# A row comparison on VectorE reads the row's number from one PSUM column in place of an SBUF constant

## Chip, cores and metric

The kernel runs on one core of a Trainium2 chip. The metric is the device time of one execution in microseconds (us). The kernel before takes 5775.4 us, the median of three runs (5774.86 to 5783.15). A profiled execution is told of separately below, because its own time is another one.

## What is computed

One message-passing layer of a graph network, with 12,500 nodes of 128 features and 412,500 edges that are sorted by `dst`. Each edge has a `src`, a `dst`, 20 attributes and a weight. Cut to what matters (ssp is softplus less log 2):

```python
h   = relu(layernorm(x)) @ W_in2f                        # 12500 x 128
Wij = (ssp(f_ij @ W_f1 + b_f1) @ W_f2 + b_f2) * rcut[:, None]
x_ij = h[dst] * Wij                                      # one row of 128 for each edge
agg = segment_sum(x_ij, src, num_segments=12500)
out = x + ssp(agg @ W_o1 + b_o1) @ W_o2 + b_o2
```

So the rows of h are picked by `dst`, which is sorted, and the products are added up by `src`, which is in no order.

## The kernel before

**Chunks and groups.** The edges are worked on in 806 chunks of 512 (`CH`), four to a group. Four tiles of 128 edges make up a chunk. A software pipeline, written out by hand in `step(k)`, takes one step for each chunk; every engine's instructions stand in the order in which `step` issues them, and nothing reorders them later. In step k the several stages work on different chunks: `blocks` on chunk k+7, `rank` on k+6, `hidden` on k+4, `window` on k+2, `value`, `pick` and `picked` on k+1, and `message` on k.

**Picking the rows of h.** As `dst` is sorted, the 512 edges of a chunk need rows out of a short window of 32 rows. h is held in DRAM in three bf16 parts, so a window is 96 rows (`WP = 3 * 32`) of 128. `rel` (96 partitions by 512 edges, bf16) has for each edge the distance of its `dst` from the window's first row, the same in each partition. The constant `prow` has in partition p the number p // 3, the row to which partition p belongs. `window` (line 748) compares the two on VectorE and so makes `at`, a matrix of zeros and ones. In `pick` (line 775) TensorE multiplies the four 96 by 128 pieces of `at` with the window `near`, into the PSUM tile `picked`. `picked` (line 783) lets ScalarE move it to `hg` in SBUF, times the edge's weight.

**Values and messages.** `hidden` (lines 658 to 662) and `hidden_end` (line 673) make the first layer of the filter net for two chunks at once, `bias` (line 760) has ScalarE write the second bias into the PSUM tile `v`, and `value` (line 767) adds the second layer to it on TensorE. `message` (line 794) multiplies `v` by `hg` on VectorE into `o`; before it, once in two chunks, line 792 copies 8 columns into a fresh buffer of `o`, of which there are four, each for two chunks.

**Slots and scatters.** `blocks` (line 678), `rank` (lines 697 and 729) and `rank_end` (line 702) work out for each edge a slot of its own in a DRAM table of its source's block of 128 nodes. `message` then has GpSimd scatter each tile of 128 rows of `o` to those slots, with one indirect DMA (line 798): four scatters to a chunk, 3224 in all. GpSimd does nothing else once the constants are made.

**Collecting.** The edges are cut into seven segments with a table each. When a segment is done, `Collect` reads its table back (`m`), compares the node in each row with the numbers 0 to 127 (`compare`, line 847) and sums the rows by a matmul (`add`, line 860), between the steps of later segments; the last segment is collected after the last step, together with the output layers. The numbers 0 to 127 of lines 678 and 847 lie in a PSUM tile, `count_ps` (allocated at line 536, and filled by ScalarE at line 1052 from the SBUF constant `places`).

**The constants.** `constants` (from line 251) makes `prow` before all of that: an iota of 96 by 512 on GpSimd (line 269), a shift on VectorE (line 294), and a copy to bf16 (line 295).

Of the kernel before, what the change touches and what calls it, by code (L numbers as in the profile page):

```python
# [9 lines left out]
F32 = mybir.dt.float32  # L10
BF16 = mybir.dt.bfloat16
F16 = mybir.dt.float16
I32 = mybir.dt.int32
AF = mybir.ActivationFunctionType
ALU = mybir.AluOpType
PSUM = bass.MemoryType.PSUM

P = 128
TG = 16
CH = 512  # L20
# [21 lines left out]
def gnn_kernel(  # L42
# [20 lines left out]
    nc = tc.nc  # L63
# [52 lines left out]
    def sbuf(name, shape, dtype=F32):  # L116
        return const.tile(shape, dtype, name=name)
# [6 lines left out]
    NC = NG * NCHUNK  # L124
    NPART = ceil_div(NC, P)
    WP = 3 * WR
# [15 lines left out]
    bf2, bo2 = (sbuf(n, [P, P]) for n in ("bf2", "bo2"))  # L142
    before = sbuf("before", [P, P])
    spare = sbuf("spare", [P, 1])
    prow = sbuf("prow", [WP, CH], BF16)
    ones = sbuf("ones", [P, 1])
    flag = sbuf("flag", [1, 1], I32)
    after = sbuf("after", [P, P], F16)
# [18 lines left out]
    early_room = state.tile([P, NTILE * P], F32, name="early_room", tag="agg")  # L167
# [4 lines left out]
    rows_at = NPART * CH * 3 // 2 + CH  # L172
# [4 lines left out]
    def early_row(k):  # L177
        return early_room[0:1, rows_at + k * NC:rows_at + (k + 1) * NC]

    first = early_row(0).bitcast(I32)  # L180
    base, last_w, strays, kept_in = (early_row(k) for k in range(1, 5))

    def load_x(q):
        n = min(QT, NTILE - q * QT)
        full = min(n, N // P - q * QT)
        xb = ln.tile([P, QT, P], F32, name="xb")
        if full < n:
            nc.vector.memset(xb[:, full:n, :], 0.0)
            nc.sync.dma_start(xb[:N % P, full, :], x[q * QN + full * P:N, :])
        if full:  # L190
            nc.sync.dma_start(xb[:, :full, :], x[q * QN:q * QN + full * P, :]
                              .rearrange("(c p) f -> p c f", p=P))
        return xb


    def first_load(i):
        h = heads[i]
        nc.sync.dma_start(first[:, h], dst_c[h, 0:1].rearrange("c o -> o c"))

    def bounds(i):  # L200

        h = heads[i]
        c0 = h.start
        while c0 < h.stop:
            t = table_of[c0]
            c1 = next((c for c in range(c0, h.stop) if table_of[c] != t), h.stop)
            nc.gpsimd.memset(base[:, c0:c1], float(tables[t][0]))
            nc.gpsimd.memset(last_w[:, c0:c1], float(tables[t][1] - WR))
            c0 = c1
# [11 lines left out]
    def part_load(k):  # L221
        c0, n = parts_c[k]
        nc.sync.dma_start(dc[k][:n, :], dst_c[c0:c0 + n, :])
# [27 lines left out]
    def constants():  # L251

        early[0] = load_x(0)
        part_load(0)
        first_load(0)
        nc.sync.dma_start(win, w_in2f)

        for j in range(NCHUNK):
            nc.sync.dma_start(wf1[32 * j:32 * j + RBF, :], w_f1)

        nc.scalar.preload_act_table_set("natural_log_exp_and_others")
        nc.scalar.dma_start(bf1, b_f1[:, None])
        nc.scalar.dma_start(wf2, w_f2)
        nc.scalar.dma_start(bf2, b_f2[None, :].to_broadcast([P, P]))
        make_identity(nc, ident)
        bounds(0)

        prow_i = early_room[:WP, rows_at + 5 * NC:rows_at + 5 * NC + CH].bitcast(I32)
        nc.gpsimd.iota(prow_i, pattern=[[0, CH]], base=0, channel_multiplier=43)
        nc.gpsimd.iota(places, pattern=[[1, P]], base=0, channel_multiplier=0,  # L270
                       allow_small_or_imprecise_dtypes=True)

        nc.gpsimd.memset(after, 1.0)
        nc.gpsimd.affine_select(out=after, in_=after, compare_op=ALU.is_ge, fill=0.0, base=-1,
                                pattern=[[1, P]], channel_multiplier=-1)
        nc.gpsimd.memset(zero, 0.0)

        nc.gpsimd.memset(before, 1.0)
        nc.gpsimd.affine_select(out=before, in_=before, compare_op=ALU.is_ge, fill=0.0, base=-1,
                                pattern=[[-1, P]], channel_multiplier=1)  # L280
        nc.gpsimd.iota(spare, pattern=[[1, 1]], base=N, channel_multiplier=1,
                       allow_small_or_imprecise_dtypes=True)
        bounds(1)
        nc.vector.memset(eps, EPS)
        nc.vector.memset(half, 0.5)
        nc.vector.memset(bad, 0.0)
        nc.vector.memset(rel[:, NPART - 1, :], 0.0)
        nc.vector.memset(ones, 1.0)
        nc.vector.memset(none, 0.0)
        nc.vector.memset(ones_b, 1.0)  # L290

        for t in range(QT):
            nc.vector.memset(turn[:, :, t:t + 1], -1.0 if t % 2 else 1.0)
        nc.vector.tensor_scalar(prow_i, prow_i, 7, None, op0=ALU.logical_shift_right)
        nc.vector.tensor_copy(prow, prow_i)
        nc.vector.scalar_tensor_tensor(after, ident, BIG, after, op0=ALU.mult, op1=ALU.add)

        nc.vector.tensor_scalar(rest_of, after, -1.0, 1.0, op0=ALU.mult, op1=ALU.add)
# [226 lines left out]
    with tc.tile_pool(name="edge", bufs=2) as edge, tc.tile_pool(  # L525
        name="quad", bufs=3
# [6 lines left out]
        free = state_ps.tile([P, CH], F32, name="free")[:, :QB]  # L533
        free_v = free.rearrange("p (t b) -> p t b", b=NBLK)

        count_ps = state_ps.tile([P, P], F32, name="count_ps")

        def clear(seg):

# [30 lines left out]
        class Group:  # L570
# [174 lines left out]
            def window(self, c):  # L745

                at = quad.tile([WP, CH], BF16, name="at")
                nc.vector.tensor_tensor(at, self.rel[:, c, :], prow, op=ALU.is_equal)  # L748
                self.at_w = at

            def bias(self, c):
# [232 lines left out]
        at = [seg.c1 + 9 for seg in segs[:-1]]  # L984
# [64 lines left out]

        with tc.manual_schedule():  # L1050
            constants()
            nc.scalar.activation(count_ps, places, AF.Copy)
            h = [make_h(q, psum) for q in range(2)]
            next(h[0])
            relative(0)
            shift(0)
            next(h[0])
            next(h[0])
            aside = side()

            start = {-9: (1, 0), -7: (2, 0), -6: (0, 1), -5: (1, 1)}
            start |= {k: (0, 1) for k in range(-4, 1)}
            for k in range(-LG, max(NCH, max(units) + 1)):
                for seg, d in zeros.get(k, ()):
                    seg.clears.append(nc.sync.dma_start(*d).ins.name)
                now = units.get(k, ())
                for c, u in now:
                    if u == 0:
                        for i in range(AHEAD):
                            c.load(i)  # L1070
                step(k, now)
                if k == -LG:
                    early[1] = load_x(1)
                for m, n in zip(h, start.get(k, (0, 0))):
                    for _ in range(n):
                        next(m, None)
                if k == -6:
                    biases(psum)
                if k >= 0:
                    next(aside, None)  # L1080
            summed[0].add(summed[1])
            summed[0].keep()
            worst = state.tile([1, 1], F32, name="worst")
            nc.vector.tensor_reduce(worst, bad, axis=mybir.AxisListType.X, op=ALU.max)
            nc.vector.tensor_copy(flag, worst)


            last = collects[-1]
            outs = []
            for b in range(0, NBLK, QT):  # L1090
                n = min(QT, NBLK - b)
                sT = kept["agg"][:, b:b + n, :].rearrange("p c f -> p (c f)")
                outs.append(finish(b, n, sT, quad, psum))

            def go(q):
                if 0 <= q < NQ:
                    next(outs[q], None)

            go(0)
            for u in range(AHEAD):  # L1100
                last.load(u)
            last.compare(0)
            q = 0
            for u in range(len(last.units)):
                last.load(u + AHEAD)
                if u + 1 < len(last.units):
                    last.compare(u + 1)
                if last.kept:
                    last.kept = []
                    go(q - 4)  # L1110
                last.add(u)
                if last.done:
                    last.keep()
                    go(q + 1)
                    go(q - 1)
                    go(q - 2)
                    go(q - 3)
                    go(q - 4)
                    q += 1
            for q in range(NQ, NQ + 5):  # L1120
                go(q - 4)
                go(q - 1)
                go(q - 2)
                go(q - 3)
                go(q - 4)

    missed = nc.values_load(flag[0:1, 0:1], min_val=0, max_val=P)
    with tc.If(missed > 0):
        with tc.tile_pool(name="any_e", bufs=2) as edge, tc.tile_pool(
            name="any_q", bufs=2  # L1130
# [51 lines left out]
```

## Time and profile before

| | |
|---|---|
| median of three runs | 5775.4 us |
| the profiled execution's own time | 4263.65 us |
| its span, from the first to the last instruction | 4261.9 us |
| TensorE busy | 3383.1 us, 79% of the span |
| VectorE busy | 3176.8 us, 75% |
| GpSimd busy | 3124.7 us, 73% |
| ScalarE busy | 2674.3 us, 63% |
| granted clock of TensorE, mean | 0.819 |
| first and last scatter start | 40.9 us and 4140.7 us |

A profiled execution is one run of the program with the hardware profiler on. Busy times, waits and durations below are from it alone, and they add up to its own time of 4263.65 us, not to the median: the profiled execution took 1512 us less than the runs that are timed without a profile. In a row of instruction groups there stand the line of the kernel, the engine, the operation, the tiles (out<-in), the shapes and the number of instructions; then the busy time in us and the mean of one in ns; then the idle time of the engine just before them, and what ended most of it.

### The profile page before, as it was taken

To read this page: it belongs to the slowest core of one execution; us is meant where nothing else is said; L and a number is where in the kernel's file an instruction comes from. 1 tells how busy PE (TensorE), PEld (TensorE's weight loads), DVE (VectorE), ACT (ScalarE), POOL (GpSimd) and SP (SyncE) were. 2 spreads that over 40 slices of the span, in tenths; PEclk is the share of its full clock that TensorE was granted. 3 is DMA by queue.
4 is the path that set the end of the run, shared out by engine and by line. 5 is a ranking of instruction groups with operands and counts; after the bars stand their busy time and mean duration, and the time that the engine had idled before them with its cause. 6 is when DMAs were issued, how large, how long until landed. Compare 5 with 4: busy or idle time off the path is not lost. (4 is left out here: it accounts for less than half of the span.)

```text
span 4261.9 us, 71875 instructions
## 1 busy us (share of the span) xinstructions
PE 3383.1 (79%) x21574; PEld 2590.7 (61%) x21574; DVE 3176.8 (75%) x6676; ACT 2674.3 (63%) x5489; POOL 3124.7 (73%) x3292
## 2 busy tenths in 40 slices
PE   6676677767777767788888888888888988988978
PEld 3444444445444444467767777777776777777767
DVE  7776666666555555667778878888888988988968
ACT  5776666666666666666666666666665666665635
POOL 5777777777777777777777777777777777777760
PEclk8867667676655665579999999999998999989989
DMA  6665655654444454467787777887787768877767
GB/s 192 189 192 166 184 172 158 180 161 137 131 124 126 120 163 123 113 183 211 232 269 206 217 208 213 248 244 212 214 238 240 234 193 269 239 203 203 196 180 223
DMA packets 515676, 820.79 MB, mean 193 GB/s; under 512 B 177170, under 2 KB 312966, under 8 KB 515282
## 3 DMA queue, kind: packets, MB, share of 16 engines
q1 hardware_dynamic: 411682, 602.85, 49.9%
q0 software_dynamic: 103168, 213.15, 15.1%
q8 instruction: 176, 2.88, 0.3%
q14 instruction: 218, 1.79, 0.1%
q10 hardware_dynamic: 432, 0.13, 0.0%
HBM read 419.09 MB, written 396.64 MB: 191 GB/s over the span
## 5 line engine op out<-in xcount | busy, mean ns | idle before, releaser
L798 POOL DMA_INDIRECT slots<-o,slot x3224 | 3117.8, 967 | 1016.2 <-issue 786.0
L767 PE MATMUL v<-wf,r 128*128 128x128 f32 x6448 | 1124.5, 330 | 374.9 <-ACT v L760 373.5
L767 PEld LDWEIGHTS v<-wf,r 128*128 128x128 f32 x6448 | 997.5, 236 | 679.4 <-ACT v L760 675.1
L760 ACT ACTIVATE v<-bf 128x512 f32<-128x512 f32 x804 | 477.5, 594 | 1387.8 <-DVE o L794 1384.1
L860 PEld LDWEIGHTS acc<-to,m 128*128 128x128 f32 x8132 | 1052.2, 207 | 348.3 <-DVE agg L883 120.7
L860 PE MATMUL acc<-to,m 128*128 128x128 f32 x8132 | 1125.4, 296 | 121.4 <-DVE agg L883 59.4
L783 ACT ACTIVATE hg<-picked,rcut 128x128 f32<-128x128 f32 x3224 | 905.5, 362 | 61.8 <-PE picked L775 59.3
L658 PE MATMUL z<-f,wf 20*128 20x512 f32 x1612 | 559.7, 771 | 336.4 <-DVE r L673 299.6
L673 DVE SCALAR_TENSOR_TENSOR r<-z,nbf,a 128x1024 f32<-128x1024 f32 x403 | 516.8, 1282 | 331.9 <-ACT a L667 331.4
L847 DVE TENSOR_TENSOR to<-count_ps,m 128x512 f32<-128x512 f32 (+3 forms) x824 | 642.6, 804 | 84.4 <-DMA m<-slots 61.2
L702 DVE TENSOR_REDUCE top<-free 128x4 f32<-128x392 f32 x806 | 448.8, 557 | 232.2 <-PE free L697 229.7
L794 DVE TENSOR_TENSOR o<-v,hg 128x512 f32<-128x512 f32 x806 | 549.8, 682 | 54.3 <-ACT hg L783 53.7
L658 PEld LDWEIGHTS z<-f,wf 20*128 20x128 f32 x1612 | 151.7, 217 | 522.5 <-issue 256.3
L667 ACT ACTIVATE a<-a,half 128x1024 f32<-128x1024 f32 x403 | 467.6, 1160 | 0.0
L661 ACT ACTIVATE a<-z,bf 128x1024 f32<-128x1024 f32 x403 | 455.1, 1129 | 9.6 <-PE z L658 9.6
L678 DVE TENSOR_TENSOR inb<-count_ps,blk 128x392 f16<-128x392 f32 x806 | 446.9, 554 | 0.0
L662 ACT ACTIVATE a<-a 128x1024 f32<-128x1024 f32 x403 | 425.9, 1057 | 12.8
L775 PE MATMUL picked<-near,at 96*128 96x128 bf16 x3224 | 377.0, 250 | 0.0
L729 PE MATMUL free<-inb,rest_of 128*128 128x392 f16 x806 | 322.1, 400 | 15.7 <-DVE top L702 15.7
L748 DVE TENSOR_TENSOR at<-rel,prow 96x512 bf16<-96x512 bf16 x806 | 332.9, 413 | 0.0
L697 PE MATMUL free<-inb,after 128*128 128x392 f16 x806 | 319.4, 396 | 3.3 <-DVE used L735 3.1
L775 PEld LDWEIGHTS <-at 96*128 96x128 bf16 x3224 | 303.7, 115 | 29.9
(109 smaller groups left out, 1141.1 us busy)
## 6 DMA issues: line engine op xcount, KB each, us to landing
m<-slots SPq DMA_DIRECT2D x311, 387.0 KB
m<-slots SPq DMA_DIRECT2D x317, 258.0 KB
rel<-rel_d SPq DMA_DIRECT2D x202, 384.0 KB
m<-slots SPq DMA_DIRECT2D x172, 322.5 KB
slots<-o,slot POOLq DMA_INDIRECT x3224
slots<-zero SPq DMA_DIRECT2D x96, 387.0 KB
slots<-zero SPq DMA_DIRECT2D x64, 516.0 KB
f<-in_f_t SPq DMA_DIRECT2D x404, 80.0 KB
```

Of the source, the lines that this page charges most:

```text
L658: nc.tensor.matmul(z[:, k, :], wf1[rows, :], self.f[rows, :], start=True, stop=True)
L661: nc.scalar.activation(a, z, AF.Abs, bias=bf1)
L667: nc.scalar.activation(a, a, AF.Ln, bias=half, scale=0.5)
L673: nc.vector.scalar_tensor_tensor(r, z, nbf1, a, op0=ALU.max, op1=ALU.add)
L760: nc.scalar.activation(v, spread(bf12, QT), AF.Copy)
L767: nc.tensor.matmul(v[:, i, :], r[:, i * P:(i + 1) * P], wf2, start=False, stop=True, skip_group_check=True)
L775: nc.tensor.matmul(ps[:, i, :], at[:, i * P:(i + 1) * P], near, start=i == 0, stop=i == QT - 1, skip_group_check=True)
L783: nc.scalar.activation(hg[:, i, :], ps[:, i, :], AF.Copy, scale=self.rcut[:, j:j + 1])
L794: nc.vector.tensor_mul(o[:, :, :P], v, hg)
L798: put = nc.gpsimd.indirect_dma_start(out=views[j % VIEWS], out_offset=bass.IndirectOffsetOnAxis(ap=self.slot[:, j:j + 1], axis=0), in_=o[: ...
L847: nc.vector.tensor_tensor(to[:, :n, :], count_ps[:, None, :].to_broadcast([P, n, P]), self.m[u][:, :n, P:].to_broadcast([P, n, P]), op=ALU ...
L860: nc.tensor.matmul(self.acc[b // QT][:, i, :], m[:, j, :P], to[:, j, :], start=t == 0, stop=t == self.seg.tiles(b) - 1)
```

## The change

`prow` shrinks from 512 columns of bf16 to one column of fp32. The PSUM tile `count_ps` is allocated with one more column, and after line 1052 ScalarE copies `prow` to that column, `prow_ps`. `window` then compares `prow_ps`, spread over 512 edges with a step of zero, with `rel`. The first operand thus comes from PSUM, and only the second from SBUF. On no engine does the order of the instructions differ; ScalarE has one more.

```diff
-    prow = sbuf("prow", [WP, CH], BF16)
+    prow = sbuf("prow", [WP, 1])
...
-        prow_i = early_room[:WP, rows_at + 5 * NC:rows_at + 5 * NC + CH].bitcast(I32)
-        nc.gpsimd.iota(prow_i, pattern=[[0, CH]], base=0, channel_multiplier=43)
+        prow_i = early_room[:WP, rows_at + 5 * NC:rows_at + 5 * NC + 1].bitcast(I32)
+        nc.gpsimd.iota(prow_i, pattern=[[0, 1]], base=0, channel_multiplier=43)
...
-        count_ps = state_ps.tile([P, P], F32, name="count_ps")
+        counts = state_ps.tile([P, P + 1], F32, name="count_ps")
+        count_ps, prow_ps = counts[:, :P], counts[:WP, P:]
...
             def window(self, c):
                 at = quad.tile([WP, CH], BF16, name="at")
-                nc.vector.tensor_tensor(at, self.rel[:, c, :], prow, op=ALU.is_equal)
+                nc.vector.tensor_tensor(at, prow_ps.to_broadcast([WP, CH]), self.rel[:, c, :],
+                                        op=ALU.is_equal)
...
             nc.scalar.activation(count_ps, places, AF.Copy)
+            nc.scalar.activation(prow_ps, prow, AF.Copy)
```

## Prediction

> **What bounds the kernel now.** I read the page first: the busy shares and the groups.
>
> ```profile
> span 4261.9 us, 71875 instructions
> ...
> PE 3383.1 (79%) x21574; PEld 2590.7 (61%) x21574; DVE 3176.8 (75%) x6676; ACT 2674.3 (63%) x5489; POOL 3124.7 (73%) x3292
> ...
> L798 POOL DMA_INDIRECT slots<-o,slot x3224 | 3117.8, 967 | 1016.2 <-issue 786.0
> ...
> L748 DVE TENSOR_TENSOR at<-rel,prow 96x512 bf16<-96x512 bf16 x806 | 332.9, 413 | 0.0
> ```
>
> By busy share GpSimd (POOL) is only third. But its 3224 scatters are busy for 3117.8 us and idle for 1016.2 us just before, and the sum, 4134.0 us, is the span from 0 to the last scatter's end. The idle time is mostly "issue", nothing that it waits for. The listing of that line's instructions shows the spread (minimum/median/maximum in ns, then first and last start in us):
>
> ```profile
> L798 POOL DMA_INDIRECT slots<-o,slot x3224: 954/958/1790, 40.9 to 4140.7; - x190
> ```
>
> From instruction to instruction, the idle time between two scatters lies between 303 and 317 ns, 304 at the median, for all 3223 pairs. So GpSimd never waits for data after its first scatter: each takes 958 + 304 = 1262 ns, and 3224 of them 4069 us of the 4101 us from the first start to the last end. **GpSimd's own pace bounds the profiled execution.** How far ahead is the rest? Pairing each multiplication of line 794 with its chunk's first scatter, I find 20 us by 160 us, 25 to 31 us from 300 to 2700 us, and 14 to 30 us after that. VectorE is in turn held back by GpSimd; of the list of waits:
>
> ```profile
> ACT v L760 <- DVE o L794: 1384.1, 456, 9.1
> ...
> DVE o L792 <- DMA slots<-o,slot: 288.0, 176, 5.1
> ```
>
> Line 792 waits for a free buffer of `o`, that is for scatters to land, 288.0 us in 176 waits, and ScalarE's long wait before `v` stands behind it.
>
> The mean scatter (967) is 9 ns over the median (958): 3224 x 9.07 = 29 us in all. Where that is lost, a stretch of the timeline shows (start us, us, what):
>
> ```profile
> 983.01 0.41 DVE L748 TENSOR_TENSOR at<-rel,prow 96x512 bf16<-96x512 bf16 x1
> 983.09 1.17 POOL L798 DMA_INDIRECT slots<-o,slot  x1 [0.30 <-issue]
> ```
>
> The scatter starts while `window` runs, and takes 1.17 us in place of 0.96. I sorted all scatters by what VectorE ran at their start and for at least 125 ns after it. For `window` there are 187, with a mean of 1079 ns: 187 x 120.8 = **22.6 us** over the median. For the lines with one operand in PSUM there is nothing: line 678 958 ns (272 scatters), 794 957 (328), 847 958 (446), 673 958 (372). Line 370, another operation with two SBUF inputs, gives 1298 (14). A delayed scatter ends as if it had been held to about 125 ns before the end of `window`.
>
> **What the Trainium skill says.** "SBUF — State Buffer", Who interferes with whom: a VectorE instruction with two SBUF inputs contends with a GpSimd instruction that reads SBUF, since its second input comes through the read interface that they share; with at most one SBUF input and outside the two-port modes there is none. The trace agrees: 1079 and 1298 ns against 957 to 958. "VectorE: DVE Perf Modes", The perf-mode tier table: tensor_tensor has a doubled rate for bf16 in SBUF and a single one with any operand in PSUM. The trace agrees, with 413 ns for 512 columns on line 748 and 682 on line 794. That page's errata section has (N + 151) / 0.96 ns for the single rate, 691 for N = 512; the trace's 682 is used.
>
> **The change, part by part.**
>
> 1. *The contention goes.* `window` keeps one SBUF input, like lines 678, 794 and 847. 187 scatters get back 120.8 ns: -22.6 us, on the bound engine, so all of it in the end time. Ends: 0, if the new form holds GpSimd as well or GpSimd isn't the bound; and -230 us, if each of the 806 windows hit a scatter for the most that it can, 411 - 125 = 286 ns. The profiled execution shows 187 hits and not 806, and so I take 22.6.
>
> 2. *`window` gets slower.* The new form isn't in the trace; its nearest rows are these, PSUM with SBUF operands (the first 512 columns, the second a comparison with a spread PSUM constant):
>
> ```profile
> L794 DVE TENSOR_TENSOR o<-v,hg 128x512 f32<-128x512 f32 x806 | 549.8, 682 | 54.3 <-ACT hg L783 53.7 <-issue 0.4
> ...
> L678 DVE TENSOR_TENSOR inb<-count_ps,blk 128x392 f16<-128x392 f32 x806 | 446.9, 554 | 0.0
> ```
>
> I take 682 (554 + 120 columns x 1/0.96 = 679 says the same; it could be 413 if the rate stayed, and not much over the page's 691). 806 x (682 - 413) = +217 us of VectorE, which becomes 3394 us, 80% of the span. On the path it costs nothing as long as GpSimd's queue of ready tiles doesn't run dry. Behind `window` on VectorE stand lines 792 and 794, then 847 and 702, each 269 ns later; behind 794 wait the scatters and ScalarE's `v`, behind that TensorE's line 767. TensorE's `pick` reads `at` a step later, with no idle time before it today. The tightest stretch is the last third:
>
> ```profile
> 2700.00:3300.00 600.00, 514.84 (x3844) 430.22 (x3843) 492.52 (x992) 370.96 (x759) 455.73 (x474) 0.93 0.78 233
> 3300.00:4142.00 842.00, 723.20 (x5451) 605.13 (x5451) 727.39 (x1426) 507.04 (x1041) 639.72 (x663) 0.93 0.74 215
> ```
>
> (Columns: stretch, us, then busy us of PE, weight loads, DVE, ACT, POOL.) VectorE is busy for 1219.9 of 1442 us, about 285 chunks; with 285 x 0.269 = 77 us more, 90%. It fits, with 14 us of ready tiles at the least to spare. Cost taken: 0; bounds 0 and the slow rival below.
>
> 3. *The constant.* The iota (549 ns), the shift (458) and the copy (424) shrink to one column, and one ScalarE copy, some 0.3 us, is added; all of them end before 5 us, the first scatter starts at 40.9. At most 0.9 us of VectorE is saved at the start, and two slower windows before the first scatter cost 0.5: taken as 0, bounds -0.9 and +0.6 us.
>
> 4. *Moved.* Nothing: no queue's order differs, and SP's DMAs are the same. No wait is added but one of `window` on ScalarE's copy, made some 27 us earlier. `count_ps` gets a third reader on VectorE, the engine that reads it already.
>
> Sum against the profiled execution: 4263.65 - 22.6 = 4241 us. The median of the timed runs is 1512 us higher, and the profile doesn't show why. If those are bound by a slower scatter, of about (5775 - 150) / 3224 = 1745 ns (150 us being the start and the tail), a window hits as often for each unit of time, but has fewer starts to hit: 22.6 x 1262 / 1745 = 16 us. If they stall more in the same place, it is more. I carry the profiled gain over unscaled: 5775.4 - 22.4 = **5753 us**. About 0.2% (12 us) is what a measurement here can tell from no change.
>
> **The rivals.**
>
> - *Nothing to tell.* What makes the timed runs 1512 us longer paces them without GpSimd's read, say a bound on TensorE, whose clock was granted at 0.819 only here. Then a gain on GpSimd is hidden: 5775. For it: the 1512 us have no place in this profile. Against: no wait of GpSimd in it. Chance 0.16.
> - *More than the profile shows.* Unprofiled, VectorE's windows and GpSimd's starts fall together more often; with every window hitting for 286 ns, 230 us: 5545. For it: a part of the 1512 us. Against: windows lie evenly over a scatter's 1262 ns, and even all hits explain 230 of 1512. Chance 0.11.
> - *Slower: VectorE becomes the bound.* In the last third its order of instructions, not its sum, decides: if its idle 222 us of 1442 are waits that a later `window` only pushes back, the 77 us are paid in full. The point from which it decides is an empty queue of ready tiles, after 14 to 25 us of loss. 77 - 25 - 22.6 = +29: 5804; from 1800 us on, where collecting begins (460 chunks, 124 us), +76: 5852. Against: VectorE's waits for landings at line 792 go on to the end, 16 us after 3300. Chance 0.12.
> - *It doesn't do what it says.* The new form holds GpSimd for its longer 682 ns: a start in the 557 ns before its last 125 is held 278 on average, 806 x 557/1262 x 278 = 99 us less 22.6: +76, 5852. The 957 to 958 ns of lines 678, 794 and 847 speak against it. Chance 0.02.
>
> **How the numbers follow.** The forecast has 0.59, with 5740 to 5765 as its own range. Range: the forecast and "nothing" hold 0.75; down to 5680 takes in the milder half of the larger gain, up to 5795 the mildest of the slow ones, 0.83 in all. Faster by over 0.2%: 0.56 of the forecast (0.03 of it falls below the limit) and 0.11, 0.67. Same: 0.16 + 0.03 = 0.19. Slower: 0.14.
>
> **What would show it.** In the profile after: the mean of line 798 down from 967 to about 960 with the median at 958; line 748 at 682 ns; no scatter over 1 us beside it, and those left beside line 370; idle time between scatters still 304 ns; VectorE busy near 3394 us, and less waiting at line 792; a span of about 4239 us. It is wrong if GpSimd waits for line 794 after the start (VectorE bounds), if long scatters stay beside `window`, or if the span falls and the timed median does not.

## The result, and the profile after

The changed kernel takes 5791.4 us (median of 22 runs, 5755.0 to 5807.4), and the kernel before takes 5773.7 us beside it (22 runs, 5751.5 to 5802.8). The ratio is 1.0023, with a 95% interval of 1.001 to 1.0035. The change did not make the kernel faster; it is slower by an amount at the limit of what can be told. (The ratios of this document come from all runs of a set, and can differ by some 0.1% from the quotient of two medians.)

The executions of this program come in two kinds, one of about 4260 us and one of 5740 to 5870 us for the kernel before; the timed runs of the kernel before were wholly of one kind in each set, and two sets on a chip of the same number, some minutes apart, were once of each kind. The profile before was of the short kind, while the three timed runs shown with it were of the long kind. Profiling itself doesn't make the difference: from here on each profiled execution is also one of the timed runs. I call the long kind *late*, for a reason that follows. The profile after is of the late kind too (its own time is 5779.0 us), so it must not be laid beside the first profile before line by line. These are its span, busy shares and groups; line 801 is now the scatter (798 before), 704 the maximum of `free` (702), 750 is `window` (748) and 797 the product `o` (794).

```profile
span 5777.2 us, 71877 instructions
...
PE 3871.4 (67%) x21574; PEld 2901.8 (50%) x21574; DVE 3378.7 (58%) x6676; ACT 2712.4 (47%) x5490; POOL 3095.3 (54%) x3292
...
L801 POOL DMA_INDIRECT slots<-o,slot x3224 | 3089.3, 958 | 2538.3 <-DVE o L797 1623.0
...
L704 DVE TENSOR_REDUCE top<-free 128x4 f32<-128x392 f32 x806 | 451.1, 560 | 1643.9 <-remote 932.7
...
L750 DVE TENSOR_TENSOR at<-count_ps,rel 96x512 bf16<-96x512 f32 x806 | 545.6, 677 | 0.0
```

Two things were forecast and are here: the mean scatter equals the median, 958 ns, and `window` takes 677 ns. But no engine is busy for more than 67% of the span, and GpSimd, which never waited for data in the first profile, is now idle for 1623.0 us until line 797 has written `o`. The list of waits (engine and line, what ended the wait; then us in total, times, longest us) says what is behind that:

```profile
POOL slots L801 <- DVE o L797: 1623.0, 359, 34.2
DVE top L704 <- remote: 932.7, 142, 11.9
...
ACT hg L786 <- remote: 851.0, 158, 10.0
```

Beside e12 below, a profile of the same kernel of the short kind, GpSimd's idle time before the scatters is 1522.7 us longer (2538.3 against 1015.6), and the span 1534.8 us: nearly all of the longer time is time in which GpSimd stands still. "remote" is a release (the signal of a semaphore that ends a wait) for which the profile shows no instruction close by. A stretch of the timeline shows one case (start us, us, what, and in brackets the idle time before and its releaser):

```profile
1272.25 0.53 PE L699 MATMUL free<-inb,after 128*128 128x392 f16 x1
...
1278.23 0.96 POOL L801 DMA_INDIRECT slots<-o,slot  x1 [0.30 <-issue]
...
1278.40 1.11 ACT L663 ACTIVATE a<-z,bf 128x1024 f32<-128x1024 f32 x1 [8.75 <-remote]
...
1282.11 0.57 DVE L704 TENSOR_REDUCE top<-free 128x4 f32<-128x392 f32 x1 [8.53 <-remote]
```

The matmul of line 699 ends at 1272.78. Line 704, which needs its result and nothing newer, starts at 1282.11, and VectorE has done nothing for 8.53 us. ScalarE is stuck in the same way for 8.75 us. GpSimd meanwhile uses up its ready tiles; its last scatter ends at 1279.19 and the next one starts 8.27 us later. So VectorE and ScalarE wait for TensorE's results although TensorE has finished them.

So that kernels can be compared, I counted such cases: an execution of line 704 that starts over 2 us after both its matmul and VectorE's previous instruction have ended. In the profile after there are 224, with 1311 us in sum; in the first profile before there is none, and the longest delay is 0.04 us. I call this sum the *lateness*. The ends of matmuls are modelled in these profiles, so one could think that the matmul itself took longer. But in 207 of the 224 cases TensorE had begun a later matmul over 2 us before line 704 started: it had gone on, and the release was late. Only 12 of the cases begin in a pause of over 0.6 us between GpSimd's scatters. In 161 such a pause begins during the case, and in each of these line 704 starts at most 3 us after GpSimd's last scatter has ended, 1.9 us at the median. Lateness thus mostly comes first, and GpSimd's empty queue after it; and the release often comes soon after the scatters have stopped. That fits the theory D below, and is no proof of it. Other engines show it too: in the late profile 629 of SyncE's instructions take 0.6 to 0.76 us, against 95 in the first profile before.

### The profile page after: what moved, and what is told of

It reads as the page before. It is cut to its first block, busy times and chain, and to the rows that moved or that the text cites. A ratio compares the mean times of both kernels' runs of the same rounds, so it can differ in the third digit from the quotient of the medians.

```text
span 5777.2 us, 71877 instructions
## 1 busy us (share of the span) xinstructions
PE 3871.4 (67%) x21574; PEld 2901.8 (50%) x21574; DVE 3378.7 (58%) x6676; ACT 2712.4 (47%) x5490; POOL 3095.3 (54%) x3292
## 3 DMA queue, kind: packets, MB, share of 16 engines
q0 software_dynamic: 103168, 213.15, 11.2%
## 5 line engine op out<-in xcount | busy, mean ns | idle before, releaser
L801 POOL DMA_INDIRECT slots<-o,slot x3224 | 3089.3, 958 | 2538.3 <-DVE o L797 1623.0
L770 PE MATMUL v<-wf,r 128*128 128x128 f32 x6448 | 1216.0, 347 | 534.8 <-issue 216.4
L863 PEld LDWEIGHTS acc<-to,m 128*128 128x128 f32 x8132 | 1228.3, 234 | 602.6 <-issue 309.2
L863 PE MATMUL acc<-to,m 128*128 128x128 f32 x8132 | 1321.9, 325 | 300.6 <-DVE agg L886 144.5
L770 PEld LDWEIGHTS v<-wf,r 128*128 128x128 f32 x6448 | 1085.3, 253 | 846.2 <-ACT v L763 336.0
L660 PE MATMUL z<-f,wf 20*128 20x512 f32 x1612 | 668.0, 881 | 401.9 <-DVE r L675 230.6
L778 PE MATMUL picked<-near,at 96*128 96x128 bf16 x3224 | 397.2, 257 | 499.2 <-ACT hg L786 323.5
L797 DVE TENSOR_TENSOR o<-v,hg 128x512 f32<-128x512 f32 x806 | 548.0, 680 | 16.9 <-ACT hg L786 12.5
L750 DVE TENSOR_TENSOR at<-count_ps,rel 96x512 bf16<-96x512 f32 x806 | 545.6, 677 | 0.0
L660 PEld LDWEIGHTS z<-f,wf 20*128 20x128 f32 x1612 | 176.4, 242 | 623.2 <-issue 421.8
L699 PE MATMUL free<-inb,after 128*128 128x392 f16 x806 | 334.6, 415 | 20.6 <-issue 16.9
```

The source lines that it names most:

```text
L660: nc.tensor.matmul(z[:, k, :], wf1[rows, :], self.f[rows, :], start=True, stop=True)
L750: nc.vector.tensor_tensor(at, prow_ps.to_broadcast([WP, CH]), self.rel[:, c, :], op=ALU.is_equal)
L770: nc.tensor.matmul(v[:, i, :], r[:, i * P:(i + 1) * P], wf2, start=False, stop=True, skip_group_check=True)
L778: nc.tensor.matmul(ps[:, i, :], at[:, i * P:(i + 1) * P], near, start=i == 0, stop=i == QT - 1, skip_group_check=True)
L797: nc.vector.tensor_mul(o[:, :, :P], v, hg)
L801: put = nc.gpsimd.indirect_dma_start(out=views[j % VIEWS], out_offset=bass.IndirectOffsetOnAxis(ap=self.slot[:, j:j + 1], axis=0), in_=o[: ...
```

## The experiments

My theory after the result (C in the expectations): without lateness the change gives what the profile promised; with lateness GpSimd runs dry and a faster scatter is worth nothing, whichever kernel runs. The rivals were that the change itself brings the lateness (B), and, for what causes it, the number of TensorE's instructions (A1), those of SyncE (A2), or the pace at which GpSimd drives the pipeline (D). The ratio is always to the kernel before in the same set of runs, and the kind is that of the kernel before there. "Held" counts scatters that start while `window` runs and at least 125 ns before its end.

| run | kernel | kind | us | before, us | ratio [95%] | lateness, us | held: number, mean ns |
|---|---|---|---|---|---|---|---|
| e1 | before | short | 4261.9 | 4260.0 | 1.0005 [0.9995, 1.0015] | 0 | 182, 1071 |
| e2 | after, one value matmul | short | 4246.9 | 4260.0 | 0.9973 [0.9963, 0.9984] | 0 | none longer |
| e3 | after, fixed window | short | 4245.3 | 4260.0 | 0.9963 [0.9949, 0.9976] | 0 | none longer |
| e4 | after | late | 5772.1 | 5764.3 | 1.0004 [0.9991, 1.0018] | 1324 | none longer |
| e5 | two SBUF inputs | late | 5667.3 | 5764.3 | 0.9844 [0.9823, 0.9865] | 1218 | 218, 1242 |
| e6 | comparison twice | late | 5852.2 | 5764.3 | 1.0135 [1.0100, 1.0169] | 1181 | none longer |
| e7 | scalar comparison | late | 5748.8 | 5764.3 | 0.9980 [0.9967, 0.9994] | 1384 | 64, 1028 |
| e8 | after | late | 5849.8 | 5841.8 | 1.0012 [0.9994, 1.0030] | 1429 | none longer |
| e9 | as e5 | late | 5755.9 | 5841.8 | 0.9869 [0.9832, 0.9907] | 1308 | 214, 1228 |
| e10 | paced by 128 columns | late | 5657.9 | 5841.8 | 0.9696 [0.9660, 0.9732] | 1170 | none longer |
| e11 | before | late | 5836.8 | 5841.8 | 0.9996 [0.9975, 1.0018] | 1476 | 108, 1059 |
| e12 | after | short | 4241.4 | 4263.3 | 0.9955 [0.9941, 0.9969] | 0 | 316, 961 (median 962): none longer |
| e13 | as e3 | short | 4243.9 | 4263.3 | 0.9955 [0.9939, 0.9972] | 0 | none longer |
| e14 | as e2 | short | 4247.3 | 4263.3 | 0.9961 [0.9946, 0.9975] | 0 | none longer |
| e15 | paced by 384 columns | short | 5222.6 | 4263.3 | 1.2250 [1.2229, 1.2270] | 0 | none longer |
| e16 | as e3 | late | 5774.4 | 5838.7 | 0.9882 [0.9852, 0.9913] | 1253 | none longer |
| e17 | as e2 | late | 5688.5 | 5838.7 | 0.9737 [0.9701, 0.9773] | 1128 | none longer |
| e18 | as e15 | late | 5210.0 | 5838.7 | 0.8922 [0.8896, 0.8948] | **0** | none longer |

**The kernel before once more (e1), and with late signals (e11).** There is no edit. Expected of e1:

> The kernel before once more, unchanged, with a profile. In the profile of the kernel after, TensorE's signals to VectorE (line 699 to line 704) come over 2 us late 224 times, 1311 us in all, and GpSimd waits 1623 us for line 797; in the first profile of the kernel before, neither occurs. Theory A (the late signals belong to nearly every execution of this program, and the first profile of before was one without them): a span near 5775 us, GpSimd idle for over 1500 us, late signals of 1200 to 1400 us in all, and scatters of about 967 ns that delay nothing. Theory B (the change brought the late signals, and what lengthens the executions of before is something else): no late signals, a span of 4262 us or one that is longer with GpSimd waiting for nothing.

Expected of e11:

> The kernel before, for a profile of it on the chip of this call. If it takes 5764 us here: 1200 to 1450 us of signals late by over 2 us from line 697 to line 702, GpSimd waiting for line 794 some 1600 us, and scatters that start in the comparison of line 748 still held to 1079 ns on average, which costs nothing there (theory C). If GpSimd never waits in it at 5764 us, theory C falls. Where it takes 4260 us, as in the first profile: no late signals, and GpSimd waiting for nothing.

e1 met executions of the short kind and repeats the first profile: 182 held scatters with a mean of 1071 ns, 20.4 us over the median in all. It could say nothing on the long kind. e11 did. Its page and list of waits:

```profile
span 5833.4 us, 71875 instructions
...
L798 POOL DMA_INDIRECT slots<-o,slot x3224 | 3103.5, 963 | 2586.9 <-DVE o L794 1673.8
```
```profile
POOL slots L798 <- DVE o L794: 1673.8, 366, 33.2
DVE top L702 <- remote: 1209.5, 176, 12.6
ACT hg L783 <- remote: 1041.4, 185, 10.3
```

The old kernel has the same waits, rather longer, and a lateness of 1476 us. The change does not bring the lateness, and B falls. The windows still hold 108 scatters there, for 10.9 us in all. That GpSimd is idle for 1673.8 us waiting for data all the same shows that its pace doesn't bound this execution.

**The kernel after, where nothing is late (e12).** No edit. Expected:

> The kernel after beside before. Where before takes 4260 us (no late signals): theory C says 4238 to 4248 us, a ratio of 0.995 to 0.997, scatters of 958 to 962 ns and GpSimd waiting for nothing after its start; theory B says no gain there either, a ratio of 0.999 or more. Where before takes 5750 to 5850: a ratio of 1.000 to 1.003, as before.

Its page:

```profile
span 4242.4 us, 71877 instructions
...
PE 3396.3 (80%) x21574; PEld 2605.8 (61%) x21574; DVE 3377.2 (80%) x6676; ACT 2682.0 (63%) x5490; POOL 3110.7 (73%) x3292
...
L801 POOL DMA_INDIRECT slots<-o,slot x3224 | 3104.6, 963 | 1015.6 <-issue 786.5
...
L750 DVE TENSOR_TENSOR at<-count_ps,rel 96x512 bf16<-96x512 f32 x806 | 545.7, 677 | 0.0
```

And of its list of waits:

```profile
DVE o L795 <- DMA slots<-o,slot: 172.7, 135, 4.3
```

This is the profile that answers to the first one. GpSimd's idle time is "issue" again, and of 3223 pairs of scatters the idle time lies between 303 and 316 ns. The 316 scatters that start beside `window` have a mean of 961 ns where the median of all is 962: they are not held. The medians differ by 21.9 us of 4263.3; the ratio of 0.9955 makes it 19 us, with 13 to 25 us as its interval. The time of 4241.4 us is the sum that the prediction made for the profiled execution.

**The kernel after again, with late signals (e4, e8).** No edit. Expected of e4:

> The kernel after once more, unchanged, beside the kernel before. Theory C (the machine, not the program, has two conditions: in one TensorE's signals come late and nothing that the change does to GpSimd or VectorE shows; in the other GpSimd's scatters pace the execution and the change is worth its lost waits): where before takes 4260 us, after takes 4238 to 4248, a ratio of 0.995 to 0.997, with scatters of 958 to 962 ns; where before takes 5775, the ratio is 1.000 to 1.004 again. Theory B (the change itself brought the late signals): 5775 us or more for after wherever before takes 4260.

Expected of e8:

> The kernel after a third time, beside before, since the chips differ: on one, before took 4260 us, on two others 5764 and 5774. Theory C (GpSimd paces the execution only where TensorE's signals come in time): if before takes 4260 us here, after takes 4238 to 4248, a ratio of 0.995 to 0.997, and GpSimd waits for nothing after its start; if before takes 5760 to 5780, a ratio of 1.000 to 1.003, and GpSimd waits for line 797 some 1600 us. Theory B (the change costs VectorE more than it gives GpSimd): a ratio over 1.002 where before takes 4260.

Neither differs from before by more than its interval. With the first result there are three ratios, 1.0004, 1.0012 and 1.0023, all at or just above 1. A gain of over 0.1% lies outside all three intervals.

**Two SBUF inputs at the new duration (e5, e9).** The one column stays in SBUF, so that duration and contention come apart:

```diff
-                nc.vector.tensor_tensor(at, prow_ps.to_broadcast([WP, CH]), self.rel[:, c, :],
+                nc.vector.tensor_tensor(at, prow.to_broadcast([WP, CH]), self.rel[:, c, :],
```

Expected of e5:

> The kernel after, with the row's number read from the fp32 column in SBUF in place of PSUM: two SBUF inputs, at the single rate, 677 ns as after. Where before takes 4260 us: if two SBUF inputs hold a scatter that starts meanwhile to about 125 ns before their end, the longer comparison hits more and for longer, 806 x 552/1262 x 276 = 97 us over the kernel after, some 4340 us, and scatters of about 990 ns on average. If GpSimd's pace had nothing to do with it (a gain that came with something else): as after, 4238 to 4250. Where before takes 5775: within 0.5% of after, as GpSimd has time to wait.

Expected of e9:

> The kernel after with the row's number from an fp32 column in SBUF once more. Where before takes 4260 us: 4310 to 4345 us, as each of the longer comparisons holds the scatters that start in it, with scatters of 980 to 990 ns, and a scatter listing without waits (theory C); as after, if two SBUF inputs cost GpSimd's pace nothing. Where before takes 5764: some 5667 again, 1.6% under before (theory D: held scatters are what makes TensorE's signals less late), or 5764 to 5790 if the first measurement came from something else.

From the page of e5:

```profile
L801 POOL DMA_INDIRECT slots<-o,slot x3224 | 3162.6, 981 | 2344.5 <-DVE o L797 1439.7
...
L750 DVE TENSOR_TENSOR at<-prow,rel 96x512 bf16<-96x512 f32 x806 | 546.6, 678 | 0.0
```

`window` takes 678 ns as in the kernel after, but now 218 scatters are held to 1242 ns, 61 us over the median in all. So it is the second SBUF input that holds GpSimd, and not the length of the instruction: the mean scatter is 981 ns where the median is 962. And yet the kernel is 1.6% faster than before, and 1.3% when repeated; the expectation for the late kind, within 0.5% of the kernel after, missed this. **Holding the engine that was thought to bound shortens the run.** That led to the theory D.

**The comparison issued twice (e6), and in a cheaper form (e7).** The edits:

```diff
+                at2 = quad.tile([WP, CH], BF16, name="at2", bufs=1)
+                nc.vector.tensor_tensor(at2, prow_ps.to_broadcast([WP, CH]), self.rel[:, c, :],
+                                        op=ALU.is_equal)
```
```diff
-                nc.vector.tensor_tensor(at, prow_ps.to_broadcast([WP, CH]), self.rel[:, c, :],
-                                        op=ALU.is_equal)
+                nc.vector.tensor_scalar(at, self.rel[:, c, :], prow, None, op0=ALU.is_equal)
```

Expected of e6:

> The kernel after, with the new comparison issued twice (the first time into a spare tile): 546 us more of VectorE, nothing more for GpSimd. Where before takes 4260 us: if VectorE has the room that the profile of before showed (it is 80% busy after), the stretch before 1800 us hides it and the rest, where 0.68 us more per chunk makes VectorE's work 5.1 to 5.2 us of GpSimd's 5.05, costs 20 to 120 us: 4260 to 4360 us, and GpSimd waits for line 797 there. If VectorE's order of instructions is the pace already after the change: 400 to 546 us more, 4640 to 4790. Where before takes 5775: more than 50 us slower than after if the 269 ns are what after lost there, less than 20 if not.

Expected of e7:

> The kernel after, with the comparison as a tensor_scalar of rel with the fp32 column as its scalar: one tensor input from SBUF and a bf16 output to SBUF[...]. Where before takes 4260 us: if [...]a scatter is hit by 806 short windows[...], 15 to 100 us over after; if, as with the short copies of before (line 792 beside 960 ns scatters), nothing shows, it is as fast as after within 0.15%. Where before takes 5775: 0 to 20 us under after[...].

e6 adds 466 us to VectorE's busy time (3844.9 against 3378.7 in the profile after) and costs 5852.2 - 5772.1 = 80 us against e4; e7 takes 246 us away (3132.4; 358 ns for one) and gains 23 us. So with late signals a us of VectorE costs 0.17 and 0.09 us by the medians, and 0.16 and 0.06 by the ratios: not nothing, and far from all. At such a price the change's 677 - 413 = 264 ns for each of 806 windows, 213 us, are worth an estimated 12 to 37 us of loss. The three ratios hold 2 to 13 us. Whether the change gives something back in the late kind, the runs don't separate.

**GpSimd paced (e10, e15, e18).** A write of zeros to an unused tile stands behind each scatter:

```diff
+    idle = sbuf("idle", [P, P])
...
+                    nc.gpsimd.memset(idle, 0.0)
```

With 128 columns (e10) the period of a scatter goes from 1263 to 1349 ns; e15 and e18 have `3 * P` columns, and 1562 to 1566 ns. Expected of e10:

> The kernel after with a memset of 128 columns on GpSimd behind each scatter, some 0.2 us, so that scatters start every 1.4 to 1.55 us at the closest in place of 1.26. Where before takes 5764 us: theory D (it is GpSimd's scatters at their full pace, five chunks at a stretch, that make TensorE's signals and SyncE's instructions late; late signals come about 2 us after GpSimd runs dry): the late signals fall by over half, and the time comes to 4900 to 5400 us. Theory E (GpSimd's runs are only a mark of the late signals, not their cause): 5780 us or more, with 1200 to 1400 us of late signals. Where before takes 4260: 150 + 3224 x 1.4 to 1.55, that is 4660 to 5150 us, as GpSimd paces there.

Expected of e15:

> The kernel after with a memset of 384 columns on GpSimd behind each scatter, about 450 ns, so that scatters start every 1.55 to 1.65 us at the closest (the memset of 128 columns made it 1.35). Where before takes 5750 to 5850 us: theory D (the pace of the scatters makes the signals late): late signals fall further, to under 900 us, and 5300 to 5600 us. If the first pacing's 3% came from something else: 5650 or more, with 1150 us of late signals or more. Where before takes 4260: 150 + 3224 x 1.55 to 1.65, that is 5150 to 5470 us.

Expected of e18:

> The kernel after, with a GpSimd write of 384 columns behind each scatter, which sets GpSimd's period to about 1.57 us (5222 us where no signal is late). Only the late condition tells. Theory D (GpSimd's pace drives the lateness, as 221 ns more of it gave 0.9696): lateness below 600 us, and a time of 5250 to 5450 us, 0.90 to 0.93 of before. Rival (lateness has its own rate for each unit of work): lateness 1100 us or more that comes on top where the queue runs dry, 5600 to 5900 us. Without lateness: 5222 us again.

e10 is 3% faster than before, and its lateness falls from 1429 us (e8, same set) to 1170. D had expected over half of it to go and 4900 to 5400 us, and its rival 5780 us or more: neither came true. e15 met the short kind, where the same kernel is simply 22.5% slower: GpSimd's pace bounds, and it was made slower. e18 then met the late kind, where the kernel before took 5838.7 us, and e16 and e17, of the same set on the same chip, had 1253 and 1128 us of lateness. Its page and waits:

```profile
span 5207.3 us, 75101 instructions
...
L802 POOL DMA_INDIRECT slots<-o,slot x3224 | 3114.9, 966 | 573.4 <-issue 503.6
...
L808 POOL MEMSET idle<- 128x384 f32 x3224 | 1402.7, 435 | 1.9
```
```profile
DVE o L796 <- DMA slots<-o,slot: 1057.9, 334, 8.0
...
POOL slots L802 <- DVE o L798: 35.7, 15, 33.4
```

Not one signal is late. GpSimd waits for data 35.7 us in place of 1623.0, nearly all of it at the start, and VectorE waits for buffers of `o` again, as in the first profile before. The time, 5210.0 us, is that of e15 within 0.3%. With a period that is 299 ns longer the kernel is 10.8% faster than before, and the paced pipeline has no late signals at all. D is shown as far as this goes: in this one set a slower pace removed the lateness. It does not show which engine's load matters, as GpSimd's pace slows all the others too.

**Fewer instructions of TensorE (e2, e14, e17) or of SyncE (e3, e13, e16).** The edits on the kernel after, which leave the results wrong: the first leaves `v` transposed, and the second always reads the window at row 0 of its table.

```diff
-                for i in range(QT):
-                    nc.tensor.matmul(v[:, i, :], r[:, i * P:(i + 1) * P], wf2,
-                                     start=False, stop=True, skip_group_check=True)
+                nc.tensor.matmul(v.rearrange("p t f -> p (t f)"), wf2, r,
+                                 start=False, stop=True, skip_group_check=True)
```
```diff
-                start = nc.sync.value_load(shifts[i][0:1, at:at + 1], min_val=0,
-                                           max_val=tables[t][1] - WR)
-                nc.sync.dma_start(self.near[c], h3_t[t][bass.ds(start, WR), :]
+                nc.sync.dma_start(self.near[c], h3_t[t][0:WR, :]
```

Expected of e2 and e3:

> The kernel after, with line 767's four fp32 matmuls of a chunk (8 weight loads and 8 matmuls in the trace) made one of 512 columns with wf2 as the weights (2 and 2): 9672 of TensorE's 43148 weight loads and matmuls go. The messages are then wrong (v comes out transposed), the waits stay as they are. Theory A1 (the late signals come from the number of TensorE's instructions): at least a fifth of the 1500 us of lateness goes, 5450 us or less. Theory A2 (they come from SyncE's stream or from the DMAs): the time stays within 1.5% of 5790 us.

> The kernel after, with the window of h read from row 0 of its table always, so that SyncE reads no row number from SBUF and computes no address: 2478 of SyncE's instructions go, some three in each chunk. The picked rows are then wrong. Theory A2 (SyncE's register instructions, 0.69 us each in the bad stretches of the profile after, make TensorE's signals late or take part in it): the late signals fall by over half and the time comes down to 4300 to 5000 us. Theory A1 (TensorE's own instructions do): the time stays within 1.5% of 5790 us, with the same late signals.

Expected of e14 and e13:

> The kernel after with one matmul of 512 columns in place of line 767's four (22% of TensorE's weight loads and matmuls less, v transposed and the messages wrong), for the condition with late signals. Where before takes 5750 to 5850 us: theory A1 (the lateness comes from the number of TensorE's instructions): 5450 us or less; theories A2 and D: within 1.5% of after. Where before takes 4260: 4247 us again, and nothing learned.

> The kernel after with the window of h read from row 0 of its table always (2478 of SyncE's instructions less, wrong rows picked), now for the condition with late signals. Where before takes 5750 to 5850 us: theory A2 (SyncE's register instructions take part in the lateness): late signals down by over a third, 5300 us or less; theory D (GpSimd's pace does) and A1 (TensorE's instructions do): within 1.5% of after. Where before takes 4260: 4245 us again, and nothing learned.

Expected of e17 and e16:

> The kernel after, with one matmul of 512 columns in place of the four of line 767 (9672 fewer TensorE instructions counting weight loads; v comes out transposed). Only the late condition tells. Theory A1 (the number of TensorE instructions makes its signals late): lateness and time fall with their share, 9672 of some 43,000, 22%: lateness near 1050 us, time 4 to 6% under before. Rival A2 or D: within 1.5% of before. Without lateness: 4245 to 4250 us, ratio 0.996.

> The kernel after, with the window of h read from the table's row 0 in place of a row number read by SyncE (2478 fewer SyncE instructions; the rows picked are then not the right ones). Only the late condition tells (before near 5800 us). Theory A2 (SyncE's register and DMA instructions, or its stalls, hold the other engines' signals): lateness below 700 us in place of 1311 to 1476, and a time 5 to 15% under before. Rival A1 or D (TensorE's own instructions, or GpSimd's pace): within 1% of before, lateness 1200 us or more. Without lateness: 4240 to 4250 us, ratio 0.995 to 0.997.

The first four met the short kind and could not tell the theories apart; they only show the change's gain again (ratios 0.9955 to 0.9973), and that 9672 fewer instructions of TensorE bring nothing where GpSimd paces. In the late kind, e16 takes 1.2% off and leaves 1253 us of lateness, where A2 had expected under 700: the 2478 instructions of SyncE are not the cause, and A2 falls. e17 takes 2.6% off and leaves 1128 us: more than the rival's 1.5% and less than the 4 to 6% of A1. TensorE's load may have a share in it; that its four matmuls became one, and so ended sooner, could explain the gain as well. In any case 22% fewer instructions of TensorE do much less than a period that is longer by 24%.

## Why the prediction was wrong, point by point

- **The bound.** "GpSimd's own pace bounds the profiled execution" is right for that execution and its kind (e12: idle time between scatters 303 to 316 ns). In the late kind, of which the timed runs are, it is wrong: GpSimd waits 1623.0 us for `o` there.
- **Part 1, the contention.** Right in cause, and in size for the short kind. In e12 no scatter is held by `window`, e5 brings them back with two SBUF inputs at 678 ns, and the gain is 21.9 us by the medians and 19 by the ratio, against 22.6. The profiles alone show less: the last scatter starts 14.6 us earlier than in the first profile (4126.1 against 4140.7), chiefly because the median scatter was 962 ns and not 958. The Trainium skill's "SBUF — State Buffer", Who interferes with whom, is borne out by 958 against 1242 ns for a scatter beside a `window` of the same duration with one and with two SBUF inputs.
- **Part 2, the slower `window`.** 677 ns against 682, and 3377.2 us of VectorE against 3394. That PSUM slows it is not shown: with the fp32 column in SBUF it takes 678 ns (e5). It was to cost nothing while GpSimd's queue doesn't run dry, and in e12 it doesn't: the waits at line 795 (792 before) shrink from 288.0 to 172.7 us, and no idle time of GpSimd between scatters is longer than 316 ns. In the last stretch VectorE comes to 1278.57 of 1428 us, 90% as forecast, from these windows of e12 (columns as before):

```profile
2700.00:3300.00 600.00, 514.97 (x3850) 431.28 (x3849) 524.31 (x1001) 372.82 (x760) 455.61 (x475) 0.93 0.77 235
3300.00:4128.00 828.00, 711.08 (x5383) 594.79 (x5383) 754.26 (x1402) 501.20 (x1028) 628.14 (x654) 0.94 0.73 214
```

- **Parts 3 and 4, the constants and the order.** Taken as 0. The first scatter starts at 40.6 us in e12 and 41.1 in the profile after, against 40.9.
- **The sum.** 4241 us against the profiled execution. e12's median is 4241.4.
- **The step that failed** is the last one: "I carry the profiled gain over unscaled". The 1512 us between profile and median were known and not explained; I assumed that they lay on GpSimd, as a slower scatter or more stalls of the same sort. In the late kind, of which the timed runs are, GpSimd is idle instead, behind late releases of TensorE's results: the kernel before has 1673.8 us of waits for `o` there (e11). While VectorE and ScalarE stand still GpSimd uses up its ready tiles, it waits for `o` 359 times in the profile after, and what a scatter saved is spent waiting. The gain carried over was 22.4 us; measured with late signals it is none (ratios 1.0004 to 1.0023). So the 4241 us that came true in e12 is right by its mechanism, and the 5753 us is wrong by its own.
- **The rivals.** "Nothing to tell" named this case: something paces the timed runs without GpSimd's read. Its example, a bound on TensorE by its granted clock, isn't it. The clock is lower in the late profile (0.719 against 0.818 in e12), but TensorE is idle for a third of the span; and e18 has a clock of 0.755 without one late signal, as e15 of the short kind has 0.750. "VectorE becomes the bound" is not what happened, as VectorE is busy for 58% of the late span; but with late signals its time is not free (e6 and e7), which the prediction's cost of 0 missed. "More than the profile shows" and "It doesn't do what it says" are excluded by the absence of held scatters in e12 and in the late profile.
- **Readings that were a little off.** GpSimd's busy and idle time before scatters, 4134.0 us, falls short of the last scatter's end at 4141.7, because GpSimd also makes constants at the start. The idle time between scatters is 305 ns at the median, not 304. At 160 us the products are some 14 us ahead of their scatters rather than 20, and from 300 to 2700 us 19 to 32. None of these moves the forecast.
- **What stays open.** Why the releases come late is not settled. It is not the change (e11), not SyncE's 2478 instructions (e16), and not TensorE's number of instructions alone (e17). It is not slower transfers either: the scatters' packets take 15.2% of the time of 16 DMA engines in e12 and 11.2% in the longer profile after, which is 645 and 647 us for each engine. A slower pace removed it (e18); and the same kernel has it in one set of runs and not in the next.

Of the versions with right results the best for the late kind is e18, 10.8% under before; where nothing is late it is the kernel after, 0.45% under before, and pacing costs 22.5% there.

## What to carry to other kernels

When the profiled execution and the timed runs differ by far more than their spread, the profile is of another machine state than the one that is judged, and no gain on its bound can be carried over before the difference has a place. Here an engine with no waits for data in the one profile had 1600 us of them in the other; a profile of a late execution of the kernel before would have shown it in one line. And an engine that runs ahead as fast as it can is not always best: where a pipeline stalls in bursts, a slower pace is worth a try, measured in the state that counts.

## What the runs showed of the hardware

- VectorE started up to 12.5 us after the matmul that it waited for had ended and VectorE itself was free (e11). In the profile after it was over 2 us late 224 times; e12, the same kernel in another set of runs, has no such case.
- The lateness depends on the pace of the pipeline: 1128 to 1476 us at median scatter periods of 1263 to 1349 ns, and none at 1562 ns (5207.3 us of span). What lies between was not measured.
- A VectorE comparison with two SBUF inputs holds an indirect scatter until some 125 ns before its end: means of 1059 to 1079 ns beside an instruction of 410 to 413 ns and of 1228 to 1242 ns beside one of 678 ns, where a free one takes 958 to 962 ns. A tensor_scalar of 358 ns held less: 64 scatters with a mean of 1028 ns (e7), where the comparison of 410 ns held 108 with a mean of 1059 ns in the same kind of run (e11).
